# Products of all column pairs: an unrolled kernel rewritten as a loop over rounds, with four pieces, two buffers and semaphores set back in stages

## The chip, the cores and the metric

The kernel runs on one core of a Trainium2 chip. The metric is the device time of one execution in microseconds (us); lower is better. Engines: DVE is VectorE, ACT is ScalarE, POOL is GpSimd, PE is TensorE (unused here), SP is SyncE, which issues the transfers. Sixteen DMA engines carry the data; every transfer of this kernel is split over all sixteen.

## The reference

```python
# r_inputs: (4096, 256) float32
def ref(inputs):
    d = inputs.shape[1]                                  # 256
    dot = jnp.einsum('bi,bj->bij', inputs, inputs)       # products within one row
    iu, ju = jnp.triu_indices(d)                         # i <= j
    return dot[:, iu, ju]                                # (4096, 32896) float32
```

Every row b of 256 numbers gives the 32,896 products x[b,i] * x[b,j] with i <= j, in the order of the upper triangle: 256 products with x[b,0], then 255 with x[b,1], down to one. The input is 4.19 MB, the output 538.97 MB.

## The kernel before

Each of the 128 partitions holds 32 rows of the input, read once into the tile `xt`. The work goes in 16 rounds of two rows per partition (`REPEAT = 2`). A round's 32,896 output columns are cut into `PIECES = 5` pieces by `even_borders`: one of 6528 columns and four of 6592. A piece is one tile `o` of 128 partitions x 2 rows x its columns, taken from a pool of three buffers (`bufs=3`), filled by ACT and DVE, and stored by one transfer that SP issues (line 164). All 16 x 5 pieces are written out one after the other in the program: the Python loops over `g` (rounds) and `c` (pieces) are unrolled. Only the very first piece is stored in four parts (`FIRST`), so that the first store can start early.

`runs` lists the triangle's rows that a piece contains: a row i is a stretch of n products with x[i] as the common factor. `split` gives the first few rows of a piece to ACT and the others to DVE: as many to ACT as bring DVE's time, by the formula in `vector_time`, down to `BUDGET` (1.08) nanoseconds per output element. ACT makes one row of one batch row per instruction (line 137): a copy with a per-partition scale. DVE has three ways, chosen in `vector_ops` by estimated time: "each", a tensor_scalar for each of the two batch rows (line 149); "all", one tensor_tensor over both batch rows with x[i] read with stride 0 (line 158); and "two", the same over two triangle rows at once. `interleave` alternates DVE's instructions between the two halves of its share.

The order of work on each engine is that of the program. A store waits for the DVE and ACT instructions that fill its buffer; the first instruction on a buffer waits for the store that last read it.

Of the kernel before, what the change touches and what calls it, by code (L numbers as in the profile page):

```python
# [1 line left out]

# [4 lines left out]

F32 = mybir.dt.float32
AF = mybir.ActivationFunctionType
ALU = mybir.AluOpType  # L10

P = 128
UNIT = 64
REPEAT = 2
PIECES = 5
BUDGET = 1.08
FIRST = [512, 1536, 3584]


def even_borders(lo: int, hi: int, pieces: int) -> list[int]:  # L20
    units = (hi - lo) // UNIT
    return [lo + units * c // pieces * UNIT for c in range(pieces)] + [hi]


def runs(d: int, lo: int, hi: int) -> list:


    found, at = [], 0
    for i in range(d):
        a, b = max(at, lo), min(at + d - i, hi)  # L30
        if a < b:
            found.append((i, i + a - at, a, b - a))
        at += d - i
    return found


def vector_ops(block: list) -> list:

    ops, k = [], 0
    while k < len(block):
        i, j, at, n = block[k]
        two = k + 2 < len(block) and i == j
        each = REPEAT * (130 + 0.52 * n)
        together = 68 + 1.046 * REPEAT * n - (34 if two else 0)
        if each <= together:
            ops.append(("each", block[k]))  # L50
        elif two:
            ops.append(("two", block[k]))
            k += 1
        else:
            ops.append(("all", block[k]))
        k += 1
    return ops


def interleave(block: list) -> list:  # L60


    half = len(block)
    while half and len(vector_ops(block[:half])) > len(vector_ops(block[half:])):
        half -= 1
    a, b = vector_ops(block[:half]), vector_ops(block[half:])
    return [op for k in range(max(len(a), len(b))) for ops in (a, b) for op in ops[k : k + 1]]


def vector_time(block: list) -> float:  # L70
    t = 0.0
    for way, (i, j, at, n) in vector_ops(block):
        if way == "each":
            t += REPEAT * (130 + 0.52 * n)
        else:
            t += 68 + 1.046 * REPEAT * n * (2 if way == "two" else 1)
    return t


def split(block: list, budget: float) -> int:  # L80


    scalar, k = 0.0, 0
    while k < len(block):
        scalar += REPEAT * (184 + 0.837 * block[k][3])
        if vector_time(block[k:]) <= budget or scalar > vector_time(block[k + 1 :]):
            break
        k += 1
    return k


def window(ap: bass.AP, free: list) -> bass.AP:
    return bass.AP(ap.tensor, ap.offset, [list(ap.ap[0]), *free])


@with_exitstack
def kernel(
    ctx: ExitStack, tc: tile.TileContext, x: bass.AP, out: bass.AP
):

    nc = tc.nc
    n, d = x.shape
    width = out.shape[1]
    assert n % (P * REPEAT) == 0 and width == d * (d + 1) // 2 and width % UNIT == 0
    groups = n // (P * REPEAT)
    borders = even_borders(0, width, PIECES)
    slot = max(b - a for a, b in zip(borders, borders[1:]))  # L110

    xpool = ctx.enter_context(tc.tile_pool(name="x", bufs=1))
    opool = ctx.enter_context(tc.tile_pool(name="o", bufs=3))

    x_in = x.rearrange("(p r) d -> p (r d)", p=P)
    x_out = out.rearrange("(p g r) c -> g p r c", p=P, r=REPEAT)


    total = n // P * d
    xt = xpool.tile([P, total + 1], F32, name="x")  # L120
    nc.vector.memset(xt[:, total:], 0.0)  # L121
    cuts = [0, REPEAT * d, total // 2, total]
    for a, b in zip(cuts, cuts[1:]):
        nc.sync.dma_start(xt[:, a:b], x_in[:, a:b])

    for g in range(groups):
        for c, (lo, hi) in enumerate(zip(borders, borders[1:])):
            o = opool.tile([P, REPEAT, slot], F32, tag="o", name=f"o_{g}_{c}")
            first = g == c == 0
            cuts = [lo, *(FIRST if first else []), hi]  # L130
            for a, b in zip(cuts, cuts[1:]):
                block = runs(d, a, b)
                k = split(block, 0.0 if first else BUDGET * REPEAT * (b - a))
                for i, j, at, length in block[:k]:
                    for r in range(REPEAT):
                        row = (g * REPEAT + r) * d
                        nc.scalar.activation(  # L137
                            o[:, r, at - lo : at - lo + length],
                            xt[:, row + j : row + j + length],
                            AF.Copy,  # L140
                            scale=xt[:, row + i : row + i + 1],
                        )
                row = g * REPEAT * d
                for way, (i, j, at, length) in interleave(block[k:]):
                    at -= lo
                    if way == "each":
                        for r in range(REPEAT):
                            row_r = row + r * d
                            nc.vector.tensor_scalar(  # L149
                                o[:, r, at : at + length],  # L150
                                xt[:, row_r + j : row_r + j + length],
                                xt[:, row_r + i : row_r + i + 1],
                                None,
                                ALU.mult,
                            )
                        continue
                    m = 2 if way == "two" else 1
                    nc.vector.tensor_tensor(  # L158
                        o[:, :, at : at + m * length],
                        window(xt[:, row + j :], [[d, REPEAT], [1, m], [1, length]]),  # L160
                        window(xt[:, row + i :], [[d, REPEAT], [1, m], [0, length]]),
                        ALU.mult,
                    )
                nc.sync.dma_start(x_out[g][:, :, a:b], o[:, :, a - lo : b - lo])  # L164


# [1 line left out]
_INS = ["r_inputs"]  # L168
_OUTS = [((4096, 32896), "float32")]


# [20 lines left out]
```

## Time and profile before

| what | value |
|---|---|
| median of 14 runs | 1277.9 us (1277.78 to 1278.05) |
| the profiled execution's own time | 1278.01 us |
| its span, first to last instruction | 1276.2 us |
| instructions in the profile | 4106 |
| DVE busy | 1128.8 us, 88% |
| ACT busy | 234.7 us, 18% |
| DMA, mean over the span | 426 GB/s |
| a store, issue to landing (median) | 33.0 us |
| SP waiting for DVE at line 164 | 979.7 us at tensor_tensor, 224.7 us at tensor_scalar |
| DVE waiting for a store | 59.3 us at line 158, 50.6 us at line 149 |

The profile's page lists first the busy time of each engine with its share of the span and its instructions, then the span in 40 equal slices with one digit per slice (tenths busy) and the rate of all DMA engines, then the DMA queues with their packets, megabytes and share of the 16 engines' time. q1 carries the kernel's transfers, q14 the instructions themselves. The chain of waits follows the work that ended last back to what released it. Windows give, for a stretch of time, its length, the busy time and instructions of DVE, ACT and POOL, the granted clock, the DMA share and GB/s. A landing record is the moment at which one DMA engine's part of a transfer is signalled as done; each transfer has 16.

### The profile page before, as it was taken

The page shows a single profiled execution, that of the slowest core. Times are in us where ns is not written, and L with a number is a line of the kernel's source. Part 1 is how long each engine was busy: PE and PEld are TensorE (multiplying, and loading weights), DVE is VectorE, ACT ScalarE, POOL GpSimd, SP SyncE. Part 2 cuts the span into 40 slices and gives each one's busy share as a digit, 9 for nine tenths or more (in the row PEclk, how much of TensorE's full clock was granted, in tenths as well). Part 3 has the DMA queues.
Part 4 walks back from the last instruction along what each step waited for, and adds up shares of the span by engine and source line. Part 5 has one row for each costly group of instructions (what it writes and reads, how often), then busy time and mean ns, then how long its engine had stood idle before and what let it go on. Part 6 is the DMA issues. An engine that isn't in the chain of part 4 may idle for free.

```text
span 1276.2 us, 4106 instructions
## 1 busy us (share of the span) xinstructions
DVE 1128.8 (88%) x2978; ACT 234.7 (18%) x787; POOL 0.2 (0%) x4
## 2 busy tenths in 40 slices
DVE  8999989898898988989889898898988989888880
ACT  4211112121121301213012130121301213012130
POOL 0000000000000000000000000000000000000000
DMA  9999999999999999999999999999999999999997
GB/s 384 432 434 430 429 432 426 432 428 432 428 430 431 426 432 428 434 427 430 428 430 432 426 433 426 434 428 429 430 430 431 427 434 428 431 429 429 432 426 314
DMA packets 23040, 543.43 MB, mean 426 GB/s; under 512 B 1376, under 2 KB 1376, under 8 KB 2016
## 3 DMA queue, kind: packets, MB, share of 16 engines
q1 hardware_dynamic: 23008, 543.17, 99.5%
q14 instruction: 32, 0.26, 0.0%
HBM read 4.19 MB, written 538.97 MB: 426 GB/s over the span
## 4 chain that ended last, share of the span: by engine, by line
DMA 62%; DVE 35%; issue 0%; DVEq 0%; SPq 0%
DMA out_dram<-o 62%; DVE o L158 24%; DVE o L149 11%; DMA x<-in_r_inputs_dram 0%; SPq L164 0%; DVEq L158 0%; DVEq L149 0%; DVEq L188 0%
## 5 line engine op out<-in xcount | busy, mean ns | idle before, releaser
L158 DVE TENSOR_TENSOR o<-x 128x104 f32<-128x104 f32 (+60 forms) x1651 | 803.8, 558 | 59.3 <-DMA out_dram<-o 59.3
L137 ACT ACTIVATE o<-x 128x197 f32<-128x197 f32 (+25 forms) x786 | 233.4, 384 | 1000.7 <-DMA out_dram<-o 919.0
L149 DVE TENSOR_SCALAR o<-x 128x216 f32<-128x216 f32 (+5 forms) x1326 | 344.5, 332 | 53.3 <-DMA out_dram<-o 50.6
L137 ACT ACT_TABLE_LOAD x1 | 1.3, 1283 | 0.7 <-PEq L179 0.7
L121 DVE MEMSET x<- 128x1 f32 x1 | 0.1, 59 | 0.8 <-PEq L179 0.8
L179 POOL MEMSET const-bfloat16-1.0<- 128x1 bf16 x1 | 0.1, 102 | 0.0
L179 POOL MEMSET const-uint8-127<- 128x1 uint8 x1 | 0.1, 102 | 0.0
L179 POOL MEMSET const-float32-1.0<- 128x1 f32 x1 | 0.1, 99 | 0.0
L179 POOL MEMSET const-float32-0.0<- 128x1 f32 x1 | 0.1, 98 | 0.2 <-issue 0.2
## 6 DMA issues: line engine op xcount, KB each, us to landing
out_dram<-o SPq DMA_DIRECT2D x64, 6592.0 KB, 33.0
out_dram<-o SPq DMA_DIRECT2D x15, 6528.0 KB, 33.3
out_dram<-o SPq DMA_DIRECT2D x1, 2944.0 KB, 17.0
x<-in_r_inputs_dram SPq DMA_DIRECT2D x1, 2048.0 KB, 12.7
out_dram<-o SPq DMA_DIRECT2D x1, 2048.0 KB, 14.0
x<-in_r_inputs_dram SPq DMA_DIRECT2D x1, 1792.0 KB, 7.2
out_dram<-o SPq DMA_DIRECT2D x1, 1024.0 KB, 11.9
out_dram<-o SPq DMA_DIRECT2D x1, 512.0 KB, 10.9
```

What stands on the lines that cost most here:

```text
L121: nc.vector.memset(xt[:, total:], 0.0)
L137: nc.scalar.activation(o[:, r, at - lo : at - lo + length], xt[:, row + j : row + j + length], AF.Copy, scale=xt[:, row + i : row + i + 1],)
L149: nc.vector.tensor_scalar(o[:, r, at : at + length], xt[:, row_r + j : row_r + j + length], xt[:, row_r + i : row_r + i + 1], None, ALU.mult,)
L158: nc.vector.tensor_tensor(o[:, :, at : at + m * length], window(xt[:, row + j :], [[d, REPEAT], [1, m], [1, length]]), window(xt[:, row + ...
L179: nc = _bacc.Bacc("TRN2", target_bir_lowering=False, num_devices=1)
```

## The change

- DVE works by tensor_tensor alone: the way "each" is gone from `vector_ops` and `vector_time`. `BUDGET` falls from 1.08 to 0.7, which gives more rows to ACT.
- A round has four pieces in place of five: three of 8448 columns and a last one of 7552 (`LAST`).
- The three buffers of one size become two tags, `o0` and `o1`, of one buffer each; pieces 0 and 2 use the first, 1 and 3 the second.
- Before each round DVE copies the round's two rows to a fixed tile `xv`, and ACT copies them to a fixed tile `xa`. All products read from these.
- The first round stays written out. Rounds 1 to 15 become a loop on the device (`tc.For_i`), whose body is one round and whose instructions are the same in every turn; only the address of the rows copied and of the stores depends on the turn.
- The loop's semaphores are set back in four stages, one per piece (`iteration_sync="staggered"`, `tc.stage_boundary()`): all engines are in adjacent stages, and a stage is entered when every engine is through the stage two before it. The heads of the loop on DVE and ACT are aligned to a block of the instruction memory.
- The output is addressed through one view per piece (`dram_disjoint_views`).

```diff
-PIECES = 5
-BUDGET = 1.08
+PIECES = 4
+LAST = 7552
+BUFS = 2
+BUDGET = 0.7
 FIRST = [512, 1536, 3584]
...
         i, j, at, n = block[k]
-        two = k + 2 < len(block) and i == j
-        each = REPEAT * (130 + 0.52 * n)
-        together = 68 + 1.046 * REPEAT * n - (34 if two else 0)
-        if each <= together:
-            ops.append(("each", block[k]))
-        elif two:
-            ops.append(("two", block[k]))
-            k += 1
-        else:
-            ops.append(("all", block[k]))
-        k += 1
+        m = 2 if k + 2 < len(block) and i == j else 1
+        ops.append((block[k], m))
+        k += m
     return ops
...
 def vector_time(block: list) -> float:
...
+    return sum(68 + 1.046 * REPEAT * n * m for (*_, n), m in vector_ops(block))
...
-    borders = even_borders(0, width, PIECES)
-    slot = max(b - a for a, b in zip(borders, borders[1:]))
+    borders = [*even_borders(0, width - LAST, PIECES - 1), width]
...
-    opool = ctx.enter_context(tc.tile_pool(name="o", bufs=3))
-
-    x_in = x.rearrange("(p r) d -> p (r d)", p=P)
-    x_out = out.rearrange("(p g r) c -> g p r c", p=P, r=REPEAT)
+    opool = ctx.enter_context(tc.tile_pool(name="o", bufs=1))
...
+    x_out = [
+        v.rearrange("(p g r) c -> g p r c", p=P, r=REPEAT)
+        for v in dram_disjoint_views(out, PIECES)
+    ]
...
+    each, total = REPEAT * d, n // P * d
+    xt = xpool.tile([P, groups, each], F32, name="x")
+    x_in = x.rearrange("(p g r) d -> p g (r d)", p=P, r=REPEAT)
+    xv = xpool.tile([P, each + 1], F32, name="xv")
+    xa = xpool.tile([P, each], F32, name="xa")
+    nc.vector.memset(xv[:, each:], 0.0)
+    cuts = [0, 1, groups // 2, groups]
...
+    def copies(x_now):
+        nc.vector.tensor_copy(xv[:, :each], x_now)
+        nc.scalar.activation(xa, x_now, AF.Copy)
+
+    def round_of_rows(g, first: bool):
         for c, (lo, hi) in enumerate(zip(borders, borders[1:])):
-            o = opool.tile([P, REPEAT, slot], F32, tag="o", name=f"o_{g}_{c}")
-            first = g == c == 0
-            cuts = [lo, *(FIRST if first else []), hi]
+            if c and not first:
+                tc.stage_boundary()
+            o = opool.tile([P, REPEAT, hi - lo], F32, tag=f"o{c % BUFS}", name=f"o{c}")
+            start = first and c == 0
+            cuts = [lo, *(FIRST if start else []), hi]
...
-                nc.sync.dma_start(x_out[g][:, :, a:b], o[:, :, a - lo : b - lo])
+                dest = x_out[c][bass.ds(g, 1), :, :, a:b].rearrange("o p r c -> p (o r) c")
+                nc.sync.dma_start(dest, o[:, :, a - lo : b - lo])
+
+    copies(xt[:, 0])
+    round_of_rows(0, first=True)
+
+    with tc.For_i(
+        1,
+        groups,
+        1,
+        hint_engines=[],
+        head_align_engines=[mybir.EngineType.DVE, mybir.EngineType.Activation],
+        iteration_sync="staggered",
+    ) as g:
+        copies(xt[:, bass.ds(g, 1)].rearrange("p o d -> p (o d)"))
+        round_of_rows(g, first=False)
```

## The prediction

> **What bounds the kernel now.** I read the page's slices and queues first, then the chain of waits, then windows over the last microseconds.
>
> ```profile
> span 1276.2 us, 4106 instructions
> DVE 1128.8 (88%) x2978; ACT 234.7 (18%) x787; POOL 0.2 (0%) x4
> ...
> DMA  9999999999999999999999999999999999999997
> ...
> q1 hardware_dynamic: 23008, 543.17, 99.5%
> q14 instruction: 32, 0.26, 0.0%
> ```
>
> DVE is at 88%, but the store queue q1 fills 99.5% of 16 DMA engines' time: the bound is the stream of stores.
>
> ```profile
> 1148.14 33.16 DMA out_dram<-o
> ...
> 1227.90 14.27 DVE o L158 x51
> ```
>
> The chain is made of such pairs: about 33 us in which a store queues and drains, then 14 us in which DVE fills the freed buffer. Two 15.7 us stores always lie ahead in the queue, so the 14 us never leave the DMA engines idle. In the trace's landing records the earliest engine finishes each 6592-column store 15.70 us after the one before: 16 packets of 26,368 bytes, 981 ns each. A round of 32,896 columns costs 4 x 15.70 + 15.55 (the 6528-column piece) = 78.35 us; sixteen rounds 1253.6. The rest is start and end.
>
> ```profile
> 1264.00:1266.00 2.00, 0.00 (x0) 0.00 (x0) 0.00 (x0) 1.00 0.98 422
> 1266.00:1268.00 2.00, 0.00 (x0) 0.00 (x0) 0.00 (x0) 1.00 0.62 264
> 1268.00:1270.00 2.00, 0.00 (x0) 0.00 (x0) 0.00 (x0) 1.00 0.09 40
> 1270.00:1272.00 2.00, 0.00 (x0) 0.00 (x0) 0.00 (x0) 1.00 0.06 26
> 1272.00:1274.00 2.00, 0.00 (x0) 0.00 (x0) 0.00 (x0) 1.00 0.09 40
> ```
>
> The columns end in DMA share and GB/s. Most engines are done by 1268; for six more microseconds 26 to 40 GB/s move, about one engine's worth. The landing records tell why: the 16 landings of a store spread over 1.0 us at the first full piece and 7.9 us at the last, growing in 23 steps that lie near packets on q14 (32 of 8 KB, 309 ns each). DVE's 3042 built instructions fill 23.8 such packets, and 23 x 0.31 is 7.1 us: the DMA engine that carries DVE's instructions falls behind by that.
>
> **What the Trainium skill says.** "Runtime: NRT & Kernel Launch", section "Instruction fetch mechanics", has instructions streamed in blocks of 256 over a DMA queue, two blocks held per engine, and a branch out of that window costing a fetch. The first half agrees: 4106 instructions at 64 bytes are the 0.26 MB of q14. No branch is in this trace. "DMA: Bandwidth & Descriptors", section "Queues, rings and completion order", says that each engine consumes its ring in order, and that an engine's semaphore increment lands after its data. The trace agrees (16 landings per store). Section "Latency and other measured facts" gives some 600 ns to the first byte; here an issue into an empty queue needed 1.02 us to the first packet and 1.31 us until all 16 engines had begun, and that is what I use. "VectorE: DVE Perf Modes", section "The perf-mode tier table", puts fp32 tensor_scalar at twice the rate of tensor_tensor; the chain has two 128x224 tensor_scalars in 0.49 us and one tensor_tensor of 856 elements in 0.96 us, so it agrees.
>
> **The change part by part.**
>
> *VectorE by tensor_tensor only, budget 0.7, four pieces.* I cost the lists of instructions with the code's formulas. For tensor_tensor, 68 ns + 1.046 ns per element gives 14.10 us for the piece that the chain has at 14.22; for ACT, 184 ns + 0.837 ns per element gives 8.10 us for thirty that the timeline has at 8.24. Pieces c = 0 to 3 then take DVE 11.7, 11.7, 12.5, 13.9 us and ACT 10.2, 11.5, 12.2, 13.2 us side by side. Stores scale with columns: 8448 are 20.1 us, 7552 are 18.0; a round stays 78.35. Gain 0: the packets grow to 33,792 bytes, but 26,112 bytes took 973 ns and 26,368 took 982, pure byte rate.
>
> *Two buffers for three.* Piece c starts when store c-2 has landed and must be issued about 1.5 us before store c-1 ends. c = 0 has 18.0 us and needs 0.6 (copy) + 11.9 + 1.5 = 14.0; c = 1: 20.1 against 13.4; c = 2: 20.1 against 14.2; c = 3: 20.1 against 15.6. The least slack is 4 us, so cost 0; what covers it is the store in flight.
>
> *Fixed copies.* An ACT copy of 512 elements is 0.61 us by the formula, a DVE copy 0.40 by the tensor_scalar one. In rounds 1 to 15 they lie inside that slack. In round 0 they move the first product by 0.4 to 0.6 us; the inputs keep the queue full to about 12 us, so most of it hides. I take +0.5, bounds -0.2 to +1.
>
> *The loop.* It removes most of the instruction stream: 118 DVE and 163 ACT instructions are repeated, under the 256 of a block. If none is fetched again, the late engine's drift goes: -7.0 us (7.9 of spread less what the engines differ by anyway), bounds -7.9 and 0.
>
> *Semaphores set back in stages.* A stage is entered when every engine, SP with its store included, is through the stage two back. That is also when the piece's buffer comes free, so the stage waits fall on waits that exist already, plus some tenths of a microsecond of slack. At the end of a round DVE is done 4 us or more before it may go on; its branch hides there, up to that much.
>
> One wait is new. In the built program's list of waits, stage 3's store raises a semaphore from 16 to 32, and SP waits for 32 on it **before it issues the next round's first store**. So the store of c = 0 is not queued behind the store of c = 3; it is issued after c = 3 has landed on all 16 engines. DVE and ACT finished c = 0 some 4 us earlier and gain nothing by it. Behind SP's wait stand the signals that admit DVE and ACT to c = 1 (slack 6 us). The DMA engines, idle 0.5% now, run empty once per round: completion packet to semaphore 0.36 us (median of 1376), SP's wake about 0.1 (the chain has 0.02 for SP's queue and 0.03 to 0.05 of issue), issue to last engine's start 1.31, together 1.77 us. The first loop round finds the semaphore already at 32, so it happens 14 times: **+24.8 us**. The trace of before has this wait nowhere (its SP waits for DVE, 979.7 us), so the bounds are 1.43 (first packet only, 20.0 us) and 2.4 us (slower issue from a register address, engines ending 0.5 us apart: 33.6 us). A gain is excluded: a queue held back can't move more.
>
> *Sum, against the profiled execution:* 1276.2 - 7.0 + 0.5 + 24.8 = 1294.5 us span. The profiled run took 1278.0, 1.8 more than its span, and the median of the runs is 0.1 below it: 1296.2, say **1296 us**, 1.4% slower.
>
> **The rivals.**
>
> *Faster: the store wait doesn't drain the queue* (it is for an older store, or the change doesn't do what its list of waits says). For it: every other wait in the loop falls on an event that the buffers need anyway. Against it: the value 32 is reached by the last store alone. Then 1276.2 - 7.0 + 0.5 + 1.7 = 1271.4 us.
>
> *No difference:* the refill costs only 0.45 us a round, a quarter of the start's, and the drift's gain pays it: 1278 us.
>
> *Slower still: instructions are fetched anew each round.* Up to four 8 KB packets on one DMA engine at 0.31 us are 1.2 us, and since each round now waits for the slowest engine this is charged 15 times: +18 us, 1314; a branch stalled beyond its 4 us would add more. Against it: both bodies fit one block.
>
> *Slower: computing is late.* Would piece 3 take over 4 us more than its 13.9, each microsecond beyond would show 15 times. DVE held the formula within 1.5% in all pieces, so this decides only with a disturbance that the trace doesn't show.
>
> **How the numbers follow.** A measurement of this kernel can tell about 0.2% (2.6 us) from no change. The drained queue has 0.78, for 1290 to 1305 (its bounds, with the drift's and the start's: 1276.2 - 7.9 - 0.2 + 20.0 + 1.7 and 1276.2 - 7.0 + 1.0 + 33.6 + 1.7); refetching, with the drain, 0.08; late computing 0.02; the faster rival 0.09; no difference 0.03. Slower is 0.88, same 0.03, faster 0.09. The range 1289 to 1310 takes in the likeliest case, with a microsecond below for what the larger packets may save (256 fewer per engine at the few ns that the durations leave open), and the lower part of refetching; it leaves out the faster case.
>
> **What would show it.** Right: the mean falls to about 420 GB/s from 426; SP waits at its store line for a store's landing some 14 times; windows of 2 us around a round's end show the DMA share fall to near zero; DVE's busy share falls to about 63%, ACT's rises to about 60%; q14 has about ten packets; the end has no six-microsecond tail. Wrong: the DMA row full at every round's end, or q14 still near 32 packets, or DVE idle at the head of a round after its buffer was free.

## The result, and the profile after

| what | before | after |
|---|---|---|
| median of the runs | 1277.86 us (1277.76 to 1278.05) | 1295.78 us (1295.70 to 1295.92) |
| the profiled execution: own time, span | 1278.01, 1276.2 us | 1295.80, 1293.6 us |
| ratio after to before | | 1.014, 95% interval 1.013 to 1.015 |

The changed kernel is 17.9 us slower, 1.4%. The forecast was 1296 us, so its total held. The experiments show that this was in part luck: the wait that the forecast names costs 6 us less than its term, and the other changes together save some 6 us less than theirs.

The page of the kernel after, slices and queues:

```profile
span 1293.6 us, 5350 instructions
DVE 813.3 (63%) x1607; ACT 772.7 (60%) x2319; POOL 0.2 (0%) x4
...
DMA  9999999999999999999999999999999999999999
GB/s 387 432 435 434 434 393 434 407 418 434 407 435 406 428 425 405 435 406 435 427 397 435 406 435 427 412 420 406 435 425 416 430 394 435 423 418 429 411 419 406
...
q1 hardware_dynamic: 18656, 543.17, 97.9%
q14 instruction: 5, 0.04, 0.0%
HBM read 4.19 MB, written 538.97 MB: 420 GB/s over the span
```

DVE and ACT are now busy for about the same time, and each is idle for more than a third of it. The row of tenths for DMA still shows 9 everywhere, because a slice of 32 us hides a gap of 1.5 us. The row of GB/s shows it: slices at 435, a stream that never stops, and between them slices at 393 to 407, which contain a round's end. The store queue has lost 1.6 points of its share, from 99.5% to 97.9%. The queue of instruction packets has 5 for 32.

SP's waits (line waited at, releaser: us in total, times, longest) say where the stream stops:

```profile
SPq L153 <- DVE o L146: 663.8, 53, 21.2
...
SPq L153 <- DMA out_dram<-o: 244.2, 14, 17.5
```

Line 153 is the store. Fifty-three times SP waits there for DVE, as it did before, with an earlier store still moving data. Fourteen times it waits for a landing. The 244.2 us are not what this costs: for most of that time the store waited for is still moving data. The cost is seen in windows around the end of the second round that the loop does (columns: the stretch, its length, busy time of DVE, ACT and POOL, clock, DMA share, GB/s; a packet is counted where it starts, so a share can pass 1):

```profile
248.00:250.00 2.00, 0.00 (x0) 0.00 (x0) 0.00 (x0) 1.00 1.12 483
250.00:252.00 2.00, 0.00 (x0) 0.02 (x1) 0.00 (x0) 1.00 0.00 0
252.00:254.00 2.00, 1.97 (x3) 2.00 (x6) 0.00 (x0) 1.00 1.27 541
```

No data packet starts between 250 and 252 us, and DVE and ACT stand still too: their work for the next store was finished before. The trace's packets give 1.52 us from the last byte of one round to the first of the next, 14 times, one every 80.12 us, and nowhere else a stretch over 0.2 us in which no engine moves data. On average it is made up of 0.49 us from the last byte to the last landing, 0.14 us until SP's store instruction starts, and 0.89 us from there to the first packet; all 16 engines have then begun within another 0.15 us.

The end of the kernel after, in the same columns:

```profile
1286.00:1288.00 2.00, 0.00 (x0) 0.00 (x0) 0.00 (x0) 1.00 1.12 483
1288.00:1290.00 2.00, 0.00 (x0) 0.00 (x0) 0.00 (x0) 1.00 1.12 483
1290.00:1292.00 2.00, 0.00 (x0) 0.00 (x0) 0.00 (x0) 1.00 0.57 242
1292.00:1293.60 1.60, 0.00 (x0) 0.00 (x0) 0.00 (x0) 1.00 0.00 0
```

The tail of six microseconds at 26 to 40 GB/s is gone: the 16 landings of the last store spread over 0.42 us, where they spread over 7.9 us before.

### The profile page after: what moved, and what is told of

It reads as the page before. It is cut to its first block, busy times and chain, and to the rows that moved or that the text cites. A ratio compares the mean times of both kernels' runs of the same rounds, so it can differ in the third digit from the quotient of the medians.

```text
span 1293.6 us, 5350 instructions
## 1 busy us (share of the span) xinstructions
DVE 813.3 (63%) x1607; ACT 772.7 (60%) x2319; POOL 0.2 (0%) x4
## 3 DMA queue, kind: packets, MB, share of 16 engines
q1 hardware_dynamic: 18656, 543.17, 97.9%
## 4 chain that ended last, share of the span: by engine, by line
DVE 60%; issue 34%; DMA 4%; DVEq 0%; SPq 0%
DVE o L146 59%; DMA out_dram<-o 4%; DVE xv L123 1%; DVEq L158 0%; DMA x<-in_r_inputs_dram 0%; DVEq L123 0%; DVEq L146 0%; SPq L153 0%
## 5 line engine op out<-in xcount | busy, mean ns | idle before, releaser
L146 DVE TENSOR_TENSOR o<-xv 128x284 f32<-128x284 f32 (+62 forms) x1590 | 806.4, 584 | 359.2 <-issue 334.1
L138 ACT ACTIVATE o<-xa 128x215 f32<-128x215 f32 (+4 forms) x2302 | 761.3, 423 | 389.9 <-issue 359.3
L124 ACT ACTIVATE xa<-x 128x512 f32 (+1 forms) x16 | 10.1, 632 | 104.7 <-issue 100.4
L123 DVE COPY xv<-x 128x512 f32 (+1 forms) x16 | 6.8, 427 | 95.6 <-issue 92.8
```

The lines of the kernel that those rows point to most:

```text
L123: nc.vector.tensor_copy(xv[:, :each], x_now)
L124: nc.scalar.activation(xa, x_now, AF.Copy)
L138: nc.scalar.activation(o[:, r, at - lo : at - lo + length], xa[:, r * d + j : r * d + j + length], AF.Copy, scale=xa[:, r * d + i : r * d ...
L146: nc.vector.tensor_tensor(o[:, :, at : at + m * length], window(xv[:, j:], [[d, REPEAT], [1, m], [1, length]]), window(xv[:, i:], [[d, REP ...
```

## The experiments

In all of them the kernel before ran beside on the same chip, at 1277.9 to 1278.0 us. The first four ask whether SP's wait is the loss, and what a loop without it takes. The spread of a store is the time from the first to the last of its 16 landings; a step is the time from a landing of one store to the same landing of the next (the first with the first, the last with the last).

**Without the wait, by another destination.** Piece 3 of rounds 1 to 15 goes to a scratch tensor, so SP has no earlier store of the output to wait for. That part of the output is left out; loop, stages, sizes and all else stay.

```diff
+    dpool = ctx.enter_context(tc.tile_pool(name="d", bufs=1, space=bass.MemoryType.DRAM))
+    scratch = dpool.tile([P, REPEAT, LAST + UNIT], F32, name="scratch")
...
+                if c == PIECES - 1 and not first:
+                    dest = scratch[:, :, :LAST]
+                else:
+                    dest = x_out[c][bass.ds(g, 1), :, :, a:b].rearrange("o p r c -> p (o r) c")
```

> The loop of the changed kernel, but in rounds 1 to 15 the last piece (c = 3) is stored to a scratch tensor in DRAM in place of the output (that part of the output is left out; same bytes, same 30,208-byte rows). The first store of a round then no longer waits for the last store of the round before; stages, branch, copies and buffers stay. Theory A (that one wait empties the store queue 14 times at 1.77 us): 1295.8 - 24.8 = 1271 us, 1269 to 1273, and no round's end with an idle DMA share. Theory B (the loop's own machinery, the hand-over of stages and the branch, delays the round's first store): unchanged, 1294 to 1297.

Measured: 1277.03 us, ratio to before 0.9993 (0.9984 to 1.0002). SP's waits at the store and the queues of this kernel:

```profile
SPq L158 <- DVE o L148: 838.3, 67, 21.3
```
```profile
q1 hardware_dynamic: 18656, 543.17, 99.3%
q14 instruction: 5, 0.04, 0.0%
```

The 14 waits for a landing at the store are gone, and with them 18.8 us: (1295.78 - 1277.03) / 14 = **1.34 us per emptied queue**. At the end of the same round as above the engines keep moving data:

```profile
248.00:250.00 2.00, 0.00 (x0) 0.00 (x0) 0.00 (x0) 1.00 1.01 438
250.00:252.00 2.00, 1.95 (x3) 2.00 (x6) 0.00 (x0) 1.00 1.21 524
```

But the time is not the 1271 us that the prediction's terms give for a loop without the wait. Its end says why:

```profile
1266.00:1268.00 2.00, 0.00 (x0) 0.00 (x0) 0.00 (x0) 1.00 0.95 408
1268.00:1270.00 2.00, 0.00 (x0) 0.00 (x0) 0.00 (x0) 1.00 0.25 106
1270.00:1272.00 2.00, 0.00 (x0) 0.00 (x0) 0.00 (x0) 1.00 0.07 30
```

Two microseconds at about one engine's rate are back: with 5 instruction packets in the whole run, one DMA engine still falls behind, and the last store's landings spread over 4.2 us. The spread grows for the first five turns and then stays at about 4 us. From there on the other engines wait too: the first landing of piece 0 comes 20.7 us after that of the store before, where 20.07 are usual. Piece 0 can't be computed before the late engine has freed its buffer: in one round it lands at 704.3 us, DVE begins at 704.8, and the store is issued at 717.4, when the other engines have almost nothing left to move. So the late engine sets the pace of all.

**Without the wait, by another loop.** The loop's semaphores are handled by registers, without stages.

```diff
-                tc.stage_boundary()
+                pass
...
-        iteration_sync="staggered",
+        iteration_sync="reg_based",
```

> The changed kernel with the loop's semaphores counted on and compared with registers in place of being set back in stages; the store waits only for its own piece's store of the round before. Everything is computed. Theory A: 1271 us, 1269 to 1273, with few instruction packets (205 DVE and 162 ACT instructions in the body). Theory B in the form that the branch costs: 1290 or more, since the branch stays; in the form that the hand-over of stages costs: 1271 too.

Measured: 1277.93 us, ratio 1.0000 (0.9991 to 1.0009); q14 has 6 packets, the spread at the end is 4.8 us. At the store SP waits 67 times for DVE and never for a landing:

```profile
SPq L153 <- DVE o L146: 1205.1, 67, 21.2
```

The whole output is stored here, and to its own place. A second loop without the wait, made in another way, comes to the same as the first within 1 us.

**No loop.** Pieces, buffers, copies and DVE's operations as after, all 16 rounds written out.

```diff
-    with tc.For_i(
...
-    ) as g:
-        copies(xt[:, bass.ds(g, 1)].rearrange("p o d -> p (o d)"))
+    for g in range(1, groups):
+        copies(xt[:, g])
```

> The changed kernel with rounds 1 to 15 written out, no loop and no stages; four pieces, two buffers, copies and tensor_tensor stay. Theory A: no emptied queue, but the instruction stream is back: ACT's 2385 instructions are 18.6 packets, 17.4 more than its first block, at 0.31 us on one DMA engine 5.4 us; 1271 + 5.4 = 1276.5 us (1275 to 1279), with a landing spread of 5 to 6 us at the end. Rival (two buffers cannot keep the queue full): 1290 or more. Rival (the drift has nothing to do with instructions): 1271 or 1278.

Measured: 1272.17 us, ratio 0.9954 (0.9938 to 0.9971). Its queues:

```profile
q1 hardware_dynamic: 18656, 543.17, 99.6%
q14 instruction: 33, 0.27, 0.1%
```

It is the fastest kernel run here, 5.7 us under before and 23.6 under after. Taking the instruction stream away was expected to save time; the version that keeps it is 4.9 us faster than the loop that has neither stream nor wait.

**More of the waits.** Without the disjoint views nearly every store of the loop waits for the landing of the one before it.

```diff
-        for v in dram_disjoint_views(out, PIECES)
+        for v in [out] * PIECES
```

> The changed kernel with the output addressed as one tensor: each store of the loop then waits for the store before it, 59 times in place of 14. Everything is computed. Theory A: 59 x 1.77 = 104.4 us, 1271 + 104.4 = 1375 us (1368 to 1382). Theory B: 1296, as the loop's machinery is the same.

Measured: 1355.18 us, ratio 1.0605 (1.0587 to 1.0622).

```profile
SPq L153 <- DVE o L146: 663.8, 53, 21.1
SPq L153 <- DMA out_dram<-o: 611.1, 59, 18.4
```

Fifty-nine waits, and (1355.18 - 1277.03) / 59 = 1.32 us each. The net price is the same at 14 and at 59 waits: the emptied queue is the cause, and it adds up wait by wait. The stretch in which no engine moves data isn't the same, 1.30 us on average for 1.52: the last landing follows the last byte after 0.37 us for 0.49, and SP's store instruction follows the landing after 0.05 for 0.14. The expectation took 1.77 us and was 20 us too high.

**What holds one engine back in the loop?** In the trace of after, one DMA engine loses some 0.25 us per round in the stretch where piece 3 is computed, its 33,792-byte packets taking about 1274 to 1293 ns where 1251 to 1258 are usual, with no instruction packet on record there after the first turns. If ACT's body, 163 instructions, fetched something at 128, two edits should change it: fewer ACT instructions, and another place of the loop's head in the instruction memory.

```diff
-BUDGET = 0.7
+BUDGET = 0.9
```

> The changed kernel with BUDGET 0.9 for 0.7: ACT's loop body falls from 163 instructions to 123, DVE's rises from 118 to some 128; the most that a piece's computing takes is about 15.2 us, still over 2 us inside its deadline. It asks what holds one DMA engine back by about 0.27 us per round while piece 3 is computed. H1, an unrecorded fetch of ACT's body when it passes 128 instructions (8 KB): the lag goes, each round is about 0.3 us shorter, 1291 us. H2, the dense short work of piece 3 itself, or anything that doesn't follow ACT's count of instructions: 1295 to 1296 us, the packets of one engine still near 1290 ns in that phase. Two emptied-queue waits of 1.3 us per round stay out of question in both: SP waits 14 times for a landing.

Measured: 1295.37 us, ratio 1.0137 (1.0120 to 1.0154): 0.4 us gained where the first theory had almost 5 (1291 us). By the landing records the engine loses 0.19 us per round for 0.25, in the same phase (leaving out the last round, in which an instruction packet falls). SP waits for a landing at the store 14 times, one for each turn but the first, as in after; the two waits per round that the expectation speaks of were a slip.

```diff
-        head_align_engines=[mybir.EngineType.DVE, mybir.EngineType.Activation],
+        head_align_engines=[mybir.EngineType.DVE],
```

> The changed kernel with ACT taken out of head_align_engines, so that ACT's loop head lies elsewhere in its block of instruction memory. H1 (a fetch at a block's border of ACT's body holds one DMA engine back): the slow packets of that engine move to another phase of the round, time about as after, 1294 to 1297 us. H2 (piece 3's dense work): the slow packets stay in piece 3's phase, 1295.8 us. A fetch that the alignment avoided and that now happens twice would show as 1299 us or more.

Measured: 1295.78 us, ratio 1.0140 (1.0123 to 1.0157), and the lag is the same, 0.26 us for 0.25, in the same phase. A fetch at a border of ACT's body is not the cause: with a body of 123 instructions and with the head elsewhere the lag stays.

**The loop that doesn't wait, with BUDGET 0.9.** The edits of the first experiment and of BUDGET are made together: piece 3 of rounds 1 to 15 goes to a scratch tensor again and is left out of the output.

> As the loop whose piece 3 goes to a scratch in rounds 1 to 15 (that part of the output is left out; it takes away what SP waits for), now with BUDGET 0.9. That kernel took 1277.0 us, where the prediction had 1271 for a loop without the wait, because one DMA engine lags by 0.45 us per round. H1 (ACT's body passing 128 instructions): the lag goes, 1271 to 1273 us. H2: 1276.5 to 1277.5 us. If the two kernels with BUDGET 0.9 differ by about 18.8 us, the emptied queue's price of 1.34 us holds with either.

Measured: 1275.41 us, ratio 0.9980 (0.9972 to 0.9988), between the two theories. The landings no longer drift apart (0.4 to 0.9 us in every round), but hardly because the late engine got faster (78.66 us per round for 78.75): DVE needs 15.1 us for piece 0 instead of 11.8, so its store comes late, all other engines run dry for about 0.5 us per round, and the late one catches up in that time. The last landing moves by 1.2 us only. Against the kernel with the wait and BUDGET 0.9 the difference is 1295.37 - 1275.41 = 20.0 us, 1.43 per wait; this pair is less clean, since piece 0's lateness counts in one of the two alone.

**Stores at fixed addresses.** All four pieces of the loop go to scratch tensors; the output of rounds 1 to 15 is left out. The edit is to the kernel of the first experiment.

```diff
-                if c == PIECES - 1 and not first:
-                    dest = scratch[:, :, :LAST]
+                if not first:
+                    dest = scratch[c][:, :, : hi - lo]
```

> As the loop whose piece 3 goes to a scratch, but all four pieces of rounds 1 to 15 go to four scratch tensors at fixed addresses (the output of these rounds is left out): no store of the loop takes its address from a register, all sizes, waits and instructions on DVE and ACT stay. That kernel took 1277.0 us, and one of its DMA engines loses 0.4 to 0.6 us per round without an instruction packet on record. If stores with an address from a register are what costs it: the lag goes, about 1271 us. If it comes from DVE's and ACT's running loop, or from the loop's semaphores: 1276.5 to 1277.5 us, and a spread of about 4 us at the end as there. Writing one place over and over may itself change the stores' pace; the step between landings of a first engine (20.07 us for 8448 columns) shows that apart.

Measured: 1276.61 us, ratio 0.9989 (0.9982 to 0.9996), spread at the end 4.0 us; the first landing's step is still 20.06 us for the full pieces 1 and 2. The stores' addresses from registers are not what costs it either. (The two copies at a round's head still take theirs from registers.)

**Two rounds per turn.** Rounds 0 and 1 are written out, and seven turns of two rounds follow, with four stages of two pieces each. The queue should run empty six times for 14. The bodies have 236 DVE and 326 ACT instructions. The second kernel takes the waits away by scratch tensors for pieces 2 and 3 of a turn's second round, which are left out of the output.

```diff
-        1,
+        2,
         groups,
-        1,
+        2,
...
+        for h in range(2):
+            if h and STAGED:
+                tc.stage_boundary()
+            copies(xt[:, bass.ds(g + h, 1)].rearrange("p o d -> p (o d)"))
+            round_of_rows(g + h, first=False)
```

> Two rounds per turn of the loop: rounds 0 and 1 are written out, seven turns follow, four stages of two pieces each. SP then waits for the last stores of a turn six times for 14. If the emptied queue is paid per wait: 6 x 1.34 = 8.0 us on a loop without it. If the other 5 us that the loop without the wait takes over the written-out version (1277.0 against 1272.2) are paid per round: 1277.0 + 8.0 = 1285.0 us. If they are paid per turn: about 1272.2 + 7 x 0.33 + 8.0 = 1282.5 us. The bodies now have some 236 DVE and 326 ACT instructions: if they are fetched again in every turn (the prediction's third rival) the instruction queue has about 35 packets for 5, on one or two DMA engines, and the time is 2 to 6 us more than the first figure.

> As the kernel with two rounds per turn, with pieces 2 and 3 of a turn's second round stored to a scratch (that part of the output is left out; it takes away what SP waits for). No emptied queue is left. Loop's other cost per round: about 1277 us. Per turn: about 1274.5 us. Against the kernel with the wait it is 8.0 us faster if 1.34 us per wait holds. Instructions fetched again, if they are, show in the instruction queue and add to the lag of one DMA engine.

Measured: 1283.66 us with the waits, ratio 1.0045 (1.0029 to 1.0062), and 1275.26 us without, ratio 0.9979 (0.9972 to 0.9987). The difference, 8.40 us, is 1.40 us for each of six waits; the packets again show six stretches of 1.5 us in which no engine moves data. SP waits for a landing at the store twelve times, but six of these waits end while other data still move. SP's waits and the queues of the kernel with the waits:

```profile
SPq L154 <- DMA out_dram<-o: 135.9, 12, 17.9
...
q1 hardware_dynamic: 18656, 543.17, 98.8%
q14 instruction: 13, 0.10, 0.0%
```

The last of the 13 instruction packets comes at 277 us, so neither body is fetched again turn by turn. The loop without the wait gains 1.8 us from having 7 turns for 15, of which 1.0 us is seen at the last landing. At most 0.2 us per turn is saved, then, and 3.1 of the 4.9 us that it loses to the written-out version stay.

**Smaller packets, no loop.** Five pieces and three buffers, as before, in the written-out version. The edit is to that version.

```diff
-PIECES = 4
-LAST = 7552
+PIECES = 5
+LAST = 6592
...
-    opool = ctx.enter_context(tc.tile_pool(name="o", bufs=1))
+    opool = ctx.enter_context(tc.tile_pool(name="o", bufs=3))
...
-            o = opool.tile([P, REPEAT, hi - lo], F32, tag=f"o{c % BUFS}", name=f"o{c}")
+            o = opool.tile([P, REPEAT, LAST], F32, tag="o", name=f"o{c}")
```

> The written-out version of the changed kernel (no loop) with five pieces of 6528 and 6592 columns and three buffers in rotation, as the kernel before has them; tensor_tensor only, copies and BUDGET 0.7 stay. If larger packets are what made the written-out version faster (33,792 against 26,368 bytes, about 0.2 us per round by the landing records): 3 us slower than it, about 1275.3 us. If piece size is nothing, as the prediction had it: 1272 us; its end spread then is what it has to show.

Measured: 1274.84 us, ratio 0.9975 (0.9966 to 0.9985): 2.7 us more than with four pieces. Number of pieces and of buffers changed together; the steps of the first landing put the difference into the stores themselves (while no engine waits, 20.08 and 17.96 us a store, 78.2 a round, where five pieces of 15.70 and 15.56 make 78.4). It is also the kernel before with only its DVE operations, split, copies and views changed, and that part alone is worth 3.0 us. Of these, 1.4 us are there by the end of round 1, and at the end the spread is 5.8 us for 7.9, with 34 instruction packets for 32; which of the changes does it wasn't tried.

**Fewer instructions, no loop.** In the written-out version with four pieces, BUDGET by piece, so that ACT has 1551 for 2319 busy instructions and DVE 1799 for 1607.

```diff
-BUDGET = 0.7
+BUDGET = [0.7, 0.9, 0.9, 1.1]
```

> The written-out version of the changed kernel with BUDGET 0.7, 0.9, 0.9 and 1.1 for pieces 0 to 3: ACT has some 1590 instructions for 2400, DVE 1780 for 1610. If the DMA engine that ends last is held back by the instructions of the engine that has most of them, 128 to a packet of 0.31 us: ACT's 18.75 packets were 5.8 us, DVE's 13.9 are 4.3 us now, so the end's spread falls from 5.0 to about 3.7 us and the time from 1272.2 to about 1271 us. If the spread has another source: no change, 1272.2 us. If computing becomes late at piece 3 (16.4 us on DVE): 1273 us or more.

Measured: 1272.51 us, ratio 0.9958 (0.9942 to 0.9975): no gain. The spread did fall, from 5.0 to 2.6 us, but not because the late engine ended earlier: the last landing moved from 1269.5 to 1269.8 us, and the first from 1264.5 to 1267.2, because piece 3's longer computing makes the others run dry. A small spread is no proof of a fast slowest engine; the last landing is what counts.

## Why the prediction was right, and where not

The landing records give one number per kernel that sums this up: the mean step of the last landing over the last 14 rounds, which is the pace of the slowest engine.

| kernel | us per round, slowest engine | median time, us |
|---|---|---|
| before | 78.77 | 1277.86 |
| written out, five pieces | 78.64 | 1274.84 |
| written out, four pieces | 78.47 | 1272.17 |
| loop without the wait (scratch; registers) | 78.75; 78.78 | 1277.03; 1277.93 |
| after | 80.11 | 1295.78 |
| wait at every store | 83.99 | 1355.18 |

After against before it is 80.11 - 78.77 = 1.34 us per round, 18.8 in 14 rounds; 1.4 us were gained by the end of round 1 (171.1 for 172.5 us). That is the 17.4 us between the spans. The run's own time is 2.2 us longer than the span in after and 1.8 before, which makes 17.8 us of it.

- **The mechanism and its count: right.** SP's wait for the last store of a turn is the loss, 14 times. Taking it away in two ways takes 18 to 19 us away, and with 6 or 59 such waits the loss is 6 or 59 times the same price.
- **The term "+24.8 us" was mis-sized: 18.8.** The prediction added 0.36 (packet to semaphore), 0.1 (SP) and 1.31 us (issue to the last engine's start, from the kernel's first transfer). At the emptied queue the trace of after has 0.49, 0.14 and 0.89 us to the first packet, 1.52 together, and all engines begin within 0.15 us, so that little is to be charged for the last one's start. A part of the 1.52 is won back: between two such stretches the slowest engine needs 80.11 - 1.52 = 78.59 us for a round, and 78.75 in the loop without the wait. Why it is faster there was not tried. The lower bound of 20.0 us was still too high by a microsecond.
- **The term "-7.0 us" for the drift failed.** The instruction packets went as foretold, 32 to 5, and so did the tail at the end. But a loop without the wait runs at 78.75 us per round, like before's 78.77: one engine loses some 0.6 us against the 78.13 (three steps of 20.07 and one of 17.92) that the others take while nothing holds them, with no instruction packet. In after this lag can't grow from round to round, since every round waits for the slowest engine; what is left of it is paid inside each round instead of at the end. Against the written-out version, which fetches its instructions all the way, the loop without the wait even loses 4.9 us. The step that failed is "if none is fetched again, the late engine's drift goes": it took the recorded packets for the whole cause.
- **"Gain 0" for operations, split and pieces was wrong by 5.7 us**, the gain of the written-out version with four pieces over before. The step from five pieces to four is 2.7 us of it. The prediction took the durations of two packet sizes for a pure byte rate; 26,112 and 26,368 bytes are 1% apart and could not show a fixed part. It did leave a microsecond open, a few nanoseconds for each of the 256 packets that an engine is spared. The other 3.0 us, from operations, split and copies, it put at nothing.
- **The start, +0.5 us:** SP issues the first store 0.8 us later (5.55 us for 4.78), but its 16 landings come no later, at 15.06 us on average for 15.15; the inputs that fill the queue hide the copies.
- **Two buffers and computing:** right for this kernel. DVE's 14.10 us and ACT's 13.34 for piece 3 were forecast at 13.9 and 13.2, and no store of after waits for them with the queue empty. In the loops without the wait the late engine does use up the slack of 4 us.

```profile
293.21 13.34 ACT L138 ACTIVATE o<-xa 128x49 f32<-128x49 f32 x48 [7.77 <-issue]
293.26 14.10 DVE L146 TENSOR_TENSOR o<-xv 128x396 f32<-128x396 f32 x51 [7.54 <-issue]
```

- **A reading beside the sum:** two tensor_scalars of 224 elements in 0.49 us and a tensor_tensor of 856 in 0.96 us take the same time per element, so these two timings don't show a factor of two. The trace of before shows it in how the times grow: from 231 to 264 ns, start to start, between 197 and 256 elements for tensor_scalar (0.56 ns per element), and from 72 to 959 ns between 2 and 856 for tensor_tensor (1.04). Nothing in the sum rests on it.
- **The rivals.** The faster one, 1271.4 us, would have been wrong even without the wait: two such loops take 1277 and 1278 us. "No difference" had 0.45 us per refill; it is 1.34. Instructions are not fetched anew each round, even with bodies twice as long.

So two errors of 6 us cancelled, by luck. By the medians, operations and tiling gain 5.69 us, the loop loses 4.86 and the wait 18.75: +17.92 in all. The prediction had +24.8 for the wait, 6 too many, and -6.5 for all the rest, where the runs have -0.8. Its sum of 1294.5 us for the span stands beside 1293.6 measured. On the kernel alone one couldn't have told; only the kernels without the wait and without the loop did.

"Runtime: NRT & Kernel Launch" in the Trainium skill, section "Instruction fetch mechanics", gives a branch out of the fetched window, which stalls, as one reason why kernels prefer full unrolling. Here the written-out version is faster, but no run shows such a stall: with the branch in place the loss is SP's wait, and a lag of one DMA engine. "DMA: Bandwidth & Descriptors", section "Anatomy of one DMA — SWDGE (gpsimd) path", has completion as most of a transfer's fixed cost, on another issuing path than this kernel's. For these stores, issued by SP, it is the other way round: at the emptied queues of after, 0.49 us from the last byte to the last landing and 0.89 us from SP's store instruction to the first packet.

What stays open is what holds one engine back in the loop. It isn't the address registers of the stores, the place of ACT's loop head, or a border in ACT's body; fewer ACT instructions lessened it a little, and half as many turns saved at most 0.2 us per turn. Under half of it (0.28 of 0.62 us per round in the loop with the scratch tensor) gathers while DVE and ACT issue piece 3's many short instructions. That was seen, not shown to be the cause.

## What to carry to other kernels

When a kernel is bound by a queue of transfers, ask of every wait on the issuing engine whether the queue still has work behind it; a wait for the last transfer queued leaves the queue empty from its last byte to the next first packet (1.5 us here), and that once per turn. Before turning an unrolled kernel into a loop, read the issuing engine's waits at the loop's head, and cost the written-out version of the same tiling as well: here all of the change's gain (5.7 us) lay in tiling and operations, and all of its loss in the loop. A forecast that hits the total has not confirmed its terms; take the main one away and see whether the rest is where the sum puts it.

## What the runs showed of the hardware

- An instruction packet of 8 KB, 309 ns long, can put one DMA engine back by more than that: in before the landings' spread jumps 23 times by 0.65 us on average, 15.0 in all, each time in a store during which such a packet moves, and 23 is about the number of packets that DVE's instructions fill. In the stores between, the late engine gains 8.2 us back (15.55 us a store for the others' 15.70). The prediction's 23 x 0.31 = 7.1 us met the net growth of 6.9 us, from 1.0 to 7.9, by luck.
- In the loops without the wait the late engine gains nothing back: its steps are 20.1 to 20.5 us for a full piece, where the others need 20.07.
- The emptied queue has about the same net price however often it comes: 1.40, 1.34 and 1.32 us at 6, 14 and 59 times, while no engine moves data for 1.50, 1.52 and 1.30 us.
